# First layer of a four-layer network on one core: key norms applied to the taps' sums, and TensorE's products regrouped by tile shape

## The chip, the cores and the metric

One Trainium2 chip, of which one core is used. The metric is the device time of one execution in microseconds (us). TensorE is called PE in the profile, VectorE DVE, ScalarE ACT, GpSimd POOL, and SyncE, which issues the DMAs, SP.

## The reference

The network has four layers, each `x = x + layer(norm(x))`, on two images of 512 channels and 64 x 64 points, in f32. Only the first layer is touched: local attention over a 3 x 3 window, with 8 heads of 64 channels, joined with attention over 256 pooled tokens.

```
q = x W_q + b_q ;  k, v = split(x W_kv + b_kv)
q_norm   = q / |q|                                  # per head and point
q_scaled = (q_norm + query_embedding) * softplus(temperature)
k_l      = k / |k|                                  # per head and point
attn_local[n, t] = q_scaled[n] . k_l[n + tap t]     # 9 taps, zero outside the image
attn_pool[n, p]  = q_scaled[n] . k_pool[p]          # 256 pooled keys
a = softmax([attn_local, attn_pool])
lt = q_norm . learnable_tokens + bias + a_local
out = sum_t lt[n, t] v[n + tap t] + a_pool v_pool   # then a projection
```

A key's inverse norm is one number per head and point, so `q . (k / |k|)` equals `(q . k) / |k|`: it can multiply the key's 64 channels, or the sum over the channels.

## The kernel before

The class `Local` computes the layer. The image's 512 channels are 4 chunks of 128 (two heads each), and each chunk's 4096 points are 4 units of 1024 points; so there are 16 units (`UT` = 1024 points, two halves of `TB` = 512). `run` works in turns. In turn i it projects keys for unit i+4 and queries for unit i+3 (each two products groups of four 128 x 128 x 512 products, L134), and values for unit i+1. It finds the inverse norms of what the turn before projected (`norms`), multiplies them in (`normed`), forms the tap products and sums of unit i+1 (`tap_products`, `tap_sums`), attends for unit i (`attend`), and weighs the values of unit i-1 (`weigh`, ten steps). Turns 1 to 11 are `steady`. Each of these is a generator, and `in_turn` takes one step of each in the order of the list `stages`. In steady turns TensorE's instructions keep the order in which they are written; the other engines, and TensorE elsewhere, are ordered by a scheduler.

- `norms`: four 128 x 32 products sum the squares per head (L2395), DVE transposes the sums, finds 1/sqrt by three Newton steps, and transposes back into rows of the buffer `sq[1]` (L2410).
- `normed`: a product of 2 rows by 128 columns spreads each row over a head's 64 channels (L2422, one pair for keys, one for queries), and DVE multiplies (L2430). For keys the result goes into `kx`, a frame of 66 x 66 points with a zero border; raw keys lie in `kraw`, queries in `qn`. `learned` (L2445) then multiplies the queries with the learnable tokens.
- `tap_products`: DVE multiplies the queries `qs` with `kx` shifted by the tap, two taps per instruction in steady turns (L2473). `tap_sums`: 128 x 32 products sum over channels into one bank `tap` (L2500), in four strips: two halves of the unit, and even and odd taps. ACT takes the exponential (L2508).
- `attend`: scores against pooled keys (L2525, 64-row products), exponentials (L2529), pooled values (L2535, 64 columns), POOL adds (L2544), sums for the softmax (L2551 and L2554, called P below), their reciprocals on DVE (L2579 to L2587), and the weights' way through a DRAM buffer `rows` (L2592).
- `weigh`: per tap, a fetch spreads the weights over 64 partitions (L2610, two DMAs, three buffers in turn), ACT copies them to a PSUM bank (L2626), DVE multiplies with the values `vx` (L2634), POOL adds (L2639).

All of SP's DMAs stand in one queue. PSUM has 5 banks named `mm` for everything here but the taps' sums and `qs`; a product can only start once its bank's last reader is done.

Of the kernel before, what the change touches and what calls it, by code (L numbers as in the profile page):

```python
# [9 lines left out]
F32 = mybir.dt.float32  # L10
I32 = mybir.dt.int32
AF = mybir.ActivationFunctionType
ALU = mybir.AluOpType
# [1954 lines left out]
class Local:  # L1968
# [9 lines left out]
    def __init__(self, net, X, Y, sp_scale, d, wp, yp, pp, ppt, pps):  # L1978
        self.net, self.nc, self.vec, self.cst = net, net.nc, net.vec, net.cst
        self.X, self.Y, self.sp_scale, self.d = X, Y, sp_scale, d  # L1980
        self.wp, self.pp, self.ppt, self.pps = wp, pp, ppt, pps
        nc, new = self.nc, lambda shape, name: wp.tile(shape, F32, name=name)

        self.yd = yp.tile([P, KC, N], F32, name="yd")
        self.wd = yp.tile([3, P, KC, C], F32, name="wd")
# [37 lines left out]
        self.qb = new([P, KC], "qe_scaled")  # L2023
        self.bias = {i: new([P, KC], "b_" + i) for i in "qkv"}
        self.raw = {"k": self.kraw, "q": self.qn}
# [20 lines left out]
    def run(self):  # L2046
# [8 lines left out]
        for i in "qkv":  # L2055
            self.fetch(i, 0)
        for i in range(-4, units + 1):
            k, q, ahead, u, before = (unit(i + n) for n in (4, 3, 1, 0, -1))
            self.steady = 1 <= i < units - 4
            streams, ended = [], []  # L2060
            stages = [self.norms(streams, ended)]
            if ahead is not None:
                stages.append(self.tap_products(ahead))
            if u is not None:
                stages.append(self.attend(u))
            if i == units:
                stages.append(self.output(KC - 2))
            if before is not None:
                stages.append(self.weigh(before))
            if ahead is not None:  # L2070
                stages.append(self.tap_sums(ahead))
            values = ([ahead] if i > 0 and ahead is not None else
                      {-4: [0], -2: [1]}.get(i, []))
            stages.append(self.projections(k, q, values, streams))
            stages.append(self.normed(ended))
            if i < -2:
                stages.append(islice(heads, 12 if i == -4 else None))
            if i == units - 3:
# [14 lines left out]
    def pooled_tokens(self):  # L2093
# [13 lines left out]
        for blk in range(NB):  # L2107
# [14 lines left out]
            if 1 <= blk <= 3:  # L2122
# [5 lines left out]
                                  self.sq[i], self.vec[:, at:at + KC])  # L2128
                nc.sync.dma_start(self.wd[i], w3)
        self.frame(self.kx)  # L2130
        return xs

    def pooled_heads(self, xs):
# [212 lines left out]
        self.net.project(ps, self.w[which], self.X, blk)  # L2346
        return ps

    def projections(self, uk, uq, uvs, streams):

        nc = self.nc

        def project(u, which, j):
# [20 lines left out]
        for step in range(10):  # L2374
            if step in made:
                i = made.index(step)
                project((uk, uq)[i // 2], "kq"[i // 2], i % 2)
            if step in taken and values:
                u, j = values.pop(0)
                self.value(u, j)  # L2380
                if j and self.last(u):
                    self.fetch("v", u // self.UN + 1)
            yield

    def norms(self, streams, ended):
# [25 lines left out]
        ended += [(s, rows[32 * s:32 * s + 2, :], *a) for s, a in enumerate(before)]  # L2411
        yield

    def normed(self, ended):

        nc = self.nc
        for _ in range(3 if self.steady else 5):
            yield
        for which in "kq":
            mine = [(e, self.bank()) for e in ended if e[2] == which]  # L2420
            for (s, rows, *_), ps in mine:
                nc.tensor.matmul(ps, self.cst[32 * s:32 * s + 2, C_ROW:C_ROW + P], rows, start=True,  # L2422
                                 stop=True)
            for (_, _, _, u, j, part, _), ps in mine:
                out = part
                if which == "k":
                    y = 1 + u % self.UN * self.UY + j * self.UY // 2
                    out = self.kx[:, y:y + self.UY // 2, 1:W + 1]
                    part, ps = (a.rearrange("p (y x) -> p y x", x=W) for a in (part, ps))
                self.multiplied = nc.vector.tensor_tensor(out, part, ps, ALU.mult).ins  # L2430
            yield
        if self.steady:
            yield
        if mine:
            self.learned(mine[-1][0][3])
        yield

    def learned(self, u):

        nc, cc, qn = self.nc, u // self.UN, self.raw["q"]  # L2440
        ps = self.bank()
        for j in range(2):
            for g in range(2):
# [8 lines left out]

    def value(self, u, j):
        ps = self.projected("v", u % self.UN * 2 + j)
        y = 1 + u % self.UN * self.UY + j * self.UY // 2
        self.nc.scalar.activation(self.vx[:, y:y + self.UY // 2, 1:W + 1],
                                  ps.rearrange("p (y x) -> p y x", x=W), AF.Identity,
                                  bias=self.bias["v"][:, u // self.UN:][:, :1])

# [2 lines left out]
    def tap_products(self, u):  # L2462
# [5 lines left out]
        for k in range(0, 9, 2) if self.steady else range(9):  # L2468
# [3 lines left out]
            with held:  # L2472
# [10 lines left out]
    def shifted(self, y, k, n):  # L2483
# [2 lines left out]
        at = lambda k: k // 3 * (W + 2) + k % 3  # L2486
        part, rows, cols = a.ap
        return bass.AP(a.tensor, a.offset + at(k), [part, [at(k + 1) - at(k), n], rows, cols])

    def tap_sums(self, u):  # L2490

# [5 lines left out]
        for k in range(9):  # L2497
            for j in range(2):
# [13 lines left out]
    def attend(self, u):  # L2512
# [58 lines left out]
            halved(1)  # L2571
        yield
        values(1)
        yield
        if not self.steady:
            yield
        psD = sums()

# [7 lines left out]
        nc.vector.tensor_tensor(el, el, self.recip, ALU.mult)  # L2586
        nc.vector.tensor_tensor(el, el, self.lt.pop(u), ALU.add)  # L2587
        if self.steady:
            yield
        self.spread = self.rows()  # L2590
        for j in range(2):
# [244 lines left out]
```

## Time and profile before

| what | value |
|---|---|
| median of 3 runs | 5038.93 us (5038.33 to 5039.80) |
| the profiled execution | 5044.18 us, its span 5042.3 us |
| busy: PE / DVE / ACT / POOL | 4811.1 / 3078.9 / 1814.7 / 1858.9 us |
| first layer's steady turns, first image | about 316 to 785 us of the span |
| period of a steady turn | 42.54 us |
| PE busy, 400 to 600 us | 196.5 of 200 us |

In a timeline a row is a group of like instructions: start, length, engine, source line, operation, tiles, tile shape (rows * columns of the array), moving operand, number of instructions, and in brackets the idle time before it with what ended it. One f32 product is two instructions on PE. A row's length holds a short overlap with its follower, so that lengths from start to start are used for sums.

### The profile page before, as it was taken

The numbers are of one execution on the slowest core, as the hardware profiler recorded it, in microseconds if no ns is written. First come the engines' busy times: TensorE is split into PE (matmuls) and PEld (weight loads), VectorE is DVE, ScalarE is ACT, GpSimd is POOL, SyncE is SP. The second block draws the span as 40 slices with busy tenths as digits, with TensorE's granted clock in tenths as the row PEclk, the third lists the DMA queues.
The fourth block names the chain that finished last, engine by engine and source line by source line (L and its number), as shares of the span: only waits on it lengthen the run. The fifth ranks groups of instructions, "written<-read, shape, count | busy, mean of one in ns | idle before, by whom it ended". The sixth has DMA issues, their size and how long they took to land. (4 is left out here: it accounts for less than half of the span.)

```text
span 5042.3 us, 48033 instructions
## 1 busy us (share of the span) xinstructions
PE 4811.1 (95%) x17027; PEld 1980.8 (39%) x17027; DVE 3078.9 (61%) x4020; ACT 1814.7 (36%) x3477; POOL 1858.9 (37%) x1218
## 2 busy tenths in 40 slices
PE   7999999999999999999999999999999999999998
PEld 3433332555334444433343333335543344444333
DVE  4267777754679633477733677777436795334776
ACT  1245555334323233322112555552443232333221
POOL 0036666501320145454500466664014101554554
PEclk9999999999999999999999999999999999999999
DMA  3035556600000000211120355565000000000111
GB/s 153 0 80 147 148 145 176 168 19 10 1 17 0 2 1 1 69 57 44 57 74 0 101 148 148 145 181 142 19 10 1 17 1 1 1 1 24 40 45 45
DMA packets 124172, 307.72 MB, mean 61 GB/s; under 512 B 20818, under 2 KB 33618, under 8 KB 122388
## 3 DMA queue, kind: packets, MB, share of 16 engines
q1 hardware_dynamic: 123924, 304.58, 20.9%
q8 instruction: 136, 2.23, 0.2%
q14 instruction: 112, 0.92, 0.1%
HBM read 256.01 MB, written 48.50 MB: 60 GB/s over the span
## 5 line engine op out<-in xcount | busy, mean ns | idle before, releaser
L134 PE MATMUL mm<-big,w 128*128 128x512 f32 x2496 | 1175.1, 614 | 30.1 <-DVE big L2430 11.7
L134 PEld LDWEIGHTS mm<-big,w 128*128 128x128 f32 x2496 | 455.3, 192 | 715.7 <-issue 553.0
L2639 POOL TENSOR_TENSOR late<-late,big 128x1024 f32<-128x1024 f32 x194 | 460.2, 2372 | 232.9 <-DVE big L2634 201.5
L2473 DVE TENSOR_TENSOR prods<-qs,big 128x1024 f32<-128x1024 f32 (+1 forms) x200 | 334.1, 1686 | 76.5 <-PE tap L2500 66.3
L1669 POOL TENSOR_TENSOR big<-big 128x512 f32<-128x512 f32 x224 | 278.0, 1273 | 219.0 <-ACT big L1660 219.0
L2634 DVE TENSOR_TENSOR big<-big,mm 128x512 f32<-128x512 f32 x388 | 254.7, 681 | 121.4 <-ACT mm L2626 120.6
L2626 ACT COPY mm<-big 128x512 f32<-128x512 f32 x432 | 248.1, 597 | 107.6 <-DMA big<-rows 59.0
L1660 ACT ACTIVATE big<-mm,ed 128x256 f32<-128x256 f32 x512 | 194.1, 490 | 233.0 <-DVE top L1656 200.3
L2544 POOL TENSOR_TENSOR late<-late 128x512 f32<-128x512 f32 x84 | 105.5, 1277 | 432.2 <-ACT late L2529 410.1
L2639 POOL TENSOR_TENSOR late<-late,tap 128x1024 f32<-128x1024 f32 x94 | 222.3, 2364 | 98.8 <-DVE tap L2634 79.9
L1472 POOL TENSOR_TENSOR wq<-prob 128x512 f32<-128x512 f32 x48 | 71.8, 1518 | 488.1 <-ACT prob L1469 476.7
L1656 DVE TENSOR_REDUCE top<-mm 128x1 f32<-128x512 f32 x256 | 159.0, 683 | 148.1 <-PE mm L1587 148.1
L1924 PE MATMUL mm<-k,w 128*128 128x512 f32 x512 | 236.6, 605 | 12.4 <-DVE k L1917 7.5
L134 PE MATMUL mm<-big,wq 128*128 128x512 f32 x512 | 236.7, 608 | 2.7 <-ACT off_t L1243 2.7
L1382 PE MATMUL acc<-big,diag 128*128 128x512 f32 x512 | 229.0, 605 | 9.8 <-ACT diag L1387 4.6
L1215 PE MATMUL mm<-big,wo 128*128 128x512 f32 x512 | 238.1, 611 | 0.0
L1634 PE MATMUL mm<-w,big 128*128 128x512 f32 x512 | 234.4, 601 | 0.0
L973 POOL TENSOR_TENSOR group_stats<-group_stats,cst 128x1 f32<-128x1 f32 (+1 forms) x20 | 20.2, 1027 | 564.6 <-DVE group_stats L972 508.2
L1914 DVE RECIPROCAL psD<-psD 128x512 f32<-128x512 f32 x64 | 215.1, 3362 | 1.9
L134 PE MATMUL mm<-big,big 128*128 128x512 f32 x464 | 201.7, 594 | 0.5 <-DVE b_sr L1011 0.5
L1469 ACT ACTIVATE prob<-mm 128x512 f32<-128x512 f32 x256 | 133.4, 602 | 171.6 <-PE mm L1466 171.3
L1556 POOL TENSOR_TENSOR sq<-k 128x512 f32<-128x512 f32 x128 | 133.1, 1042 | 155.2 <-ACT k L1554 139.1
(425 smaller groups left out, 8219.2 us busy)
## 6 DMA issues: line engine op xcount, KB each, us to landing
big<-rows SPq DMA_DIRECT2D x432, 256.0 KB, 4.2
tap<-rows SPq DMA_DIRECT2D x208, 256.0 KB, 4.1
yd<-late SPq DMA_DIRECT2D x32, 512.0 KB, 3.1
lost_all<-lost SPq DMA_DIRECT2D x128, 128.0 KB, 3.1
out<-big SPq DMA_DIRECT2D x64, 256.0 KB, 2.0
big<-in_W_kv SPq DMA_DIRECT2D x8, 1024.0 KB, 10.3
rows<-late SPq DMA_DIRECT2D x64, 128.0 KB, 3.6
big<-in_x SPq DMA_DIRECT2D x32, 256.0 KB, 3.6
```

Of the source, the lines that this page charges most:

```text
L134: self.nc.tensor.matmul(ps, w[:, kc, :], X[:, kc, blk * TB:(blk + 1) * TB], start=(kc == 0), stop=(kc == KC - 1))
L1215: nc.tensor.matmul(ps, w[:, kc, oc * P:(oc + 1) * P], att[:, kc, :], start=(kc == 0), stop=(kc == KC - 1))
L1382: nc.tensor.matmul(accs[b], dg, src[:, b * TB:(b + 1) * TB], start=(j == 0), stop=(j == 6))
L1634: nc.tensor.matmul(ps, X[:, kc, lo:lo + P], wv[:, kc, :], start=(kc == 0), stop=(kc == KC - 1))
L1660: nc.scalar.activation(f[:, t, :], pS[h][i][:, t % 2, :], AF.Exp, bias=ed[:, t, 2 * cc + h:2 * cc + h + 1])
L1669: nc.gpsimd.tensor_tensor(a, a, part, ALU.add)
L1914: nc.vector.reciprocal(psD, psD)
L1924: nc.tensor.matmul(ps, self.wo[:, kc, oc * P:(oc + 1) * P], qs[:, kc, :], start=(kc == 0), stop=(kc == KC - 1))
L2473: self.nc.vector.tensor_tensor(self.pair(u, k)[:, :n].rearrange("p k (y x) -> p k y x", x=W), bcast(qs.rearrange("p (y x) -> p y x", x=W), ...
L2626: nc.scalar.copy(ps, part)
L2634: nc.vector.tensor_tensor(part.rearrange("p (y x) -> p y x", x=W), self.vx[:, y:y + self.UY // 2, dx:dx + W], ps.rearrange("p (y x) -> p y ...
L2639: nc.gpsimd.tensor_tensor(out, out, t, ALU.add)
```

## The change

Keys are no longer multiplied by their inverse norms. ACT writes the raw projected keys straight into `kx`. The inverse norms of keys go by DMA into a DRAM buffer `inverse`, per chunk six rows (three copies of two heads), with zeros at both ends. `tap_inverses` reads them back in twelve DMAs of 6 rows x 512, each shifted as its taps are, into a 128 x 512 buffer (the place of `kraw`), and DVE multiplies the taps' sums by it in PSUM before the exponential. Keys are projected one turn later, with the queries of the same unit. In steady turns the stages' order and their steps are moved: `norms` after `attend`, tap sums of taps 4 to 7 in one step next to the learned product, pooled values next to the sums, and the three projections of the last steps behind one another.

```diff
@@ run
-            k, q, ahead, u, before = (unit(i + n) for n in (4, 3, 1, 0, -1))
+            made, ahead, u, before = (unit(i + n) for n in (3, 1, 0, -1))
...
-            stages = [self.norms(streams, ended)]
+            norms = self.norms(streams, ended)
+            stages = [] if self.steady else [norms]
...
                 stages.append(self.attend(u))
+            if self.steady:
+                stages.append(norms)
...
-            stages.append(self.projections(k, q, values, streams))
-            stages.append(self.normed(ended))
+            last = [self.projections(made, values, streams), self.normed(ended)]
+            stages += reversed(last) if self.steady else last
@@ pooled_tokens
+        nc.gpsimd.memset(self.kraw[:, :TB], 0.0)
+        for at in (0, self.edge - 1 + N):
+            nc.sync.dma_start(self.inverse[:, at:at + self.edge + 1],
+                              self.cst[:6 * KC, :self.edge + 1])
@@ projections
-            part = self.raw[which][:, j * TB:(j + 1) * TB]
-            nc.scalar.activation(part, ps, AF.Identity, bias=b)
+            if which == "q":
+                part = self.qn[:, j * TB:(j + 1) * TB]
+                nc.scalar.activation(part, ps, AF.Identity, bias=b)
+            else:
+                part = None
+                nc.scalar.activation(self.rows_of(self.kx, u, j),
+                                     ps.rearrange("p (y x) -> p y x", x=W), AF.Identity, bias=b)
@@ norms
+        for s, (which, u, j, part, _) in enumerate(before):
+            row = rows[32 * s:32 * s + 2, :]
+            if which == "q":
+                ended.append((s, row, u, j, part))
+                continue
+            at = self.edge + 1 + u % self.UN * self.UT + j * TB
+            a = self.inverse[u // self.UN * 6:][:2, at:at + TB]
+            heads, cols = a.ap
+            nc.sync.dma_start(bass.AP(a.tensor, a.offset, [heads, [2 * heads[0] - 1, 3], cols]),
+                              bcast(row, 1, 3))
@@ normed
-        for which in "kq":
-            mine = [(e, self.bank()) for e in ended if e[2] == which]
...
+        mine = [(e, self.bank()) for e in ended]
...
+        for (*_, part), ps in mine:
+            self.multiplied = nc.vector.tensor_tensor(part, part, ps, ALU.mult).ins
+        for _ in range(2):
             yield
@@ tap_products
-            for _ in range(n):
+            for _ in range(1 if self.steady and k > 2 else n):
                 yield
@@ tap_inverses (new)
+        inverse = (self.kraw[:, :TB] if u < KC * self.UN - 1
+                   else self.w3[:, 2].rearrange("p k o -> p (k o)"))
+        for q in range(4):
+            for dy in range(3):
+                at = u % self.UN * self.UT + q // 2 * TB + dy * W + 1
+                self.nc.sync.dma_start(inverse[32 * q + 6 * dy:][:6, :],
+                                       self.inverse[u // self.UN * 6:][:6, at:at + TB])
+        return inverse
@@ tap_sums
+            if k == 3:
+                inverse = self.tap_inverses(u)
             if k % 2:
-                for _ in range(((2, 2, 3, 1) if self.steady else (2, 2, 2, 1))[k // 2]):
+                for _ in range(((2, 2, 0, 1) if self.steady else (2, 2, 2, 1))[k // 2]):
                     yield
+        nc.vector.tensor_tensor(ps, ps, inverse, ALU.mult)
         el = self.els()
         nc.scalar.activation(el, ps, AF.Exp)
@@ attend, after values(1)
-        yield
         if not self.steady:
             yield
+            yield
         psD = sums()
...
         if self.steady:
+            yield
             yield
         self.spread = self.rows()
```

In the changed kernel these lines have other numbers: L2395 becomes L2413, L2422 L2448, L2430 L2451, L2473 L2492, L2500 L2530, L2525 L2558, L2535 L2568, L2551 and L2554 L2584 and L2587, L2634 L2668; new are L2437 (write of inverse norms), L2516 (read) and L2539 (the multiply of the sums).

More of the change, by code (lines that the diff above doesn't have):

```diff
@@ L1984, in __init__ @@
         self.yd = yp.tile([P, KC, N], F32, name="yd")
+        self.edge = W + 1
+        self.inverse = yp.tile([6 * KC, N + 2 * self.edge], F32, name="inverse")
         self.wd = yp.tile([3, P, KC, C], F32, name="wd")
@@ L2024, in __init__ @@
         self.bias = {i: new([P, KC], "b_" + i) for i in "qkv"}
-        self.raw = {"k": self.kraw, "q": self.qn}
         self.w, self.lt, self.el, self.out = {}, {}, {}, {}
@@ L2347, in projected, with rows_of, projections, project @@
         return ps
-    def projections(self, uk, uq, uvs, streams):
+    def rows_of(self, a, u, j):
+        y = 1 + u % self.UN * self.UY + j * self.UY // 2
+        return a[:, y:y + self.UY // 2, 1:W + 1]
+    def projections(self, u, uvs, streams):
         nc = self.nc
-        def project(u, which, j):
+        def project(which, j):
             if u is None:
@@ L2376, in projections @@
                 i = made.index(step)
-                project((uk, uq)[i // 2], "kq"[i // 2], i % 2)
+                project("kq"[i // 2], i % 2)
             if step in taken and values:
[L2379 to L2382, printed above, removed]
+                v, j = values.pop(0)
+                self.value(v, j)
+                if j and self.last(v):
+                    self.fetch("v", v // self.UN + 1)
             yield
@@ L2410, in norms @@
         nc.vector.transpose(rows, ps)
-        ended += [(s, rows[32 * s:32 * s + 2, :], *a) for s, a in enumerate(before)]
+        for s, (which, u, j, part, _) in enumerate(before):
[8 more added lines that the diff above has]
+                              bcast(row, 1, 3))
         yield
@@ L2418, in normed @@
             yield
-        for which in "kq":
-            mine = [(e, self.bank()) for e in ended if e[2] == which]
[L2421 to L2430, printed above, removed]
-            yield
-        if self.steady:
+        mine = [(e, self.bank()) for e in ended]
+        for (s, rows, *_), ps in mine:
+            nc.tensor.matmul(ps, self.cst[32 * s:32 * s + 2, C_ROW:C_ROW + P], rows, start=True,
+                             stop=True)
+        for (*_, part), ps in mine:
+            self.multiplied = nc.vector.tensor_tensor(part, part, ps, ALU.mult).ins
+        for _ in range(2):
             yield
         if mine:
-            self.learned(mine[-1][0][3])
+            self.learned(mine[-1][0][2])
         yield
     def learned(self, u):
-        nc, cc, qn = self.nc, u // self.UN, self.raw["q"]
+        nc, cc, qn = self.nc, u // self.UN, self.qn
         ps = self.bank()
@@ L2454, in value @@
         ps = self.projected("v", u % self.UN * 2 + j)
-        y = 1 + u % self.UN * self.UY + j * self.UY // 2
-        self.nc.scalar.activation(self.vx[:, y:y + self.UY // 2, 1:W + 1],
+        self.nc.scalar.activation(self.rows_of(self.vx, u, j),
                                   ps.rearrange("p (y x) -> p y x", x=W), AF.Identity,
@@ L2488, in shifted, with tap_inverses @@
         return bass.AP(a.tensor, a.offset + at(k), [part, [at(k + 1) - at(k), n], rows, cols])
+    def tap_inverses(self, u):
+        inverse = (self.kraw[:, :TB] if u < KC * self.UN - 1
[6 more added lines that the diff above has]
+        return inverse
     def tap_sums(self, u):
@@ L2573, in attend @@
         values(1)
-        yield
         if not self.steady:
+            yield
             yield
```

## The prediction

> **What bounds the kernel now.** I read the page's 40 slices first, then the busy time by stretch, then TensorE's own timeline.
>
> ```profile
> PE   7999999999999999999999999999999999999998
> L134 PE MATMUL mm<-big,w 128*128 128x512 f32 x2496 | 1175.1, 614 | 30.1 <-DVE big L2430 11.7
> ```
>
> ```profile
> 400.00:600.00 200.00, 196.51 (x719) 61.21 (x718) 151.03 (x235) 119.15 (x212) 122.90 (x63) 1.00 0.55 149
> ```
>
> TensorE (PE) is busy in every slice, and in the first layer's middle for 196.5 of 200 us, against 151.0 for VectorE (DVE), 119.2 for ScalarE (ACT) and 122.9 for GpSimd (POOL). So TensorE's work and its switches are what counts there, but DVE at 76% can become the next bound. One turn of the steady stage, in TensorE's timeline (start, length, group; two instructions make one f32 product):
>
> ```profile
> 544.36 1.06 PE L2500 MATMUL tap<-prods,cst 128*32 128x512 f32 x8
> 545.35 1.13 PE L2422 MATMUL mm<-sq,cst 2*128 2x512 f32 x4
> 546.41 1.13 PE L2525 MATMUL mm<-big,kp 64*128 64x512 f32 x4
> 548.06 3.70 PE L134 MATMUL mm<-big,w 128*128 128x512 f32 x8 [0.53 <-DVE big L2430]
> 551.70 1.13 PE L2422 MATMUL mm<-sq,cst 2*128 2x512 f32 x4
> 552.75 1.94 PE L2535 MATMUL mm<-late,vp 128*64 128x512 f32 x8
> ...
> 558.49 3.70 PE L134 MATMUL mm<-big,w 128*128 128x512 f32 x8
> 562.12 1.06 PE L2445 MATMUL mm<-big 128*32 128x512 f32 x8
> 563.12 3.70 PE L134 MATMUL mm<-big,w 128*128 128x512 f32 x8
> 566.75 1.07 PE L2500 MATMUL tap<-prods,cst 128*32 128x512 f32 x8
> ```
>
> The same groups return every 42.54 us (548.06, then 590.61). Almost all follow without a gap; a turn's gaps are 0.53 us (on DVE) and 0.17 us (on ACT), so 41.84 us of a turn is TensorE's own. There are 23 groups of differing tile shape in a turn.
>
> [...] two neighbouring groups of one shape are shorter than two apart.
>
> ```profile
> 274.85 7.13 PE L134 MATMUL mm<-big,w 128*128 128x512 f32 x16
> 826.98 1.92 PE L2500 MATMUL tap<-prods,cst 128*32 128x512 f32 x16
> ```
>
> Two projections apart take 2 x 3.63 us from start to start, side by side 7.06 (274.85 to 281.91): 0.20 us less. Two tap groups apart take 2 x 1.00, side by side about 1.86 (1.92 less the overlap of 0.07 at its end): 0.14 less. [...] ACT's copies of taps stand behind activations that wait for PE (DVE L2634 waits up to 2.4 us for them). [...] the 16 KB write `lost<-half` lands after 1.9 us.
>
> **The change, part by part.** I took the order of instructions and each wait's producer from the changed program as built, and all durations from the profile of before.
>
> *Keys' scaling.* 64 of the 128 L2422 products go: 32 pairs of 1.06 us, 11 in each image's steady turns and 5 outside. 64 DVE multiplies of 0.68 us go and 32 come (L2539, tap sums times inverse norms, 0.7 us by the like L2634): DVE gains 0.7 us a turn. New on SP's queue: in each turn 2 writes of inverse norms and 12 reads of 12 KB. A tap fetch takes 0.55 us to issue[...].
>
> *Side by side.* In a steady turn the projections stand in 4 groups, not 6 (2 x 0.20); the 32-column products in 3, not 7 (4 x 0.14); the last values join the sums (0.16). That is 1.12 us; with the keys' pair 2.18. TensorE's own turn becomes 41.84 - 2.18 = 39.66 us.
>
> *New waits.* The turn's end is now: sums (P), tap products 4 to 7 with the learned product, tap 8, three projections (k1, q0, q1). q1 needs the PSUM bank of weighing step 7, so DVE's multiply of that step. DVE's list after P, with lengths from this view:
>
> ```profile
> 558.61 0.73 DVE L2579 STREAM_TRANSPOSE mm<-mm 128x512 f32<-128x512 f32 x1 [0.20 <-PE mm L2554]
> 559.37 0.37 DVE L2581 RECIPROCAL mm<-mm 128x32 f32<-128x32 f32 x1
> 559.77 0.72 DVE L2582 STREAM_TRANSPOSE late<-mm 128x512 f32<-128x512 f32 x1
> 560.53 0.95 DVE L2586 TENSOR_TENSOR late<-late 128x512 f32<-128x512 f32 x1
> 561.51 0.69 DVE L2587 TENSOR_TENSOR late<-late 128x512 f32<-128x512 f32 x1
> ...
> 567.88 2.29 DVE L2473 TENSOR_TENSOR prods<-qs,big 128x2048 f32<-128x2048 f32 x1 [1.40 <-PE tap L2500]
> ```
>
> From P's end: transpose and reciprocal 1.2; tap product 8 (1.2, it waits for the products of 4 and 5) 2.4; transpose 3.1; weighing step 6 and the two small ops 5.9; the next unit's first pair (2.2) 8.1; L2539 8.8; second pair 11.0; only then step 7, done at 11.7. In before, step 7 came ahead of these pairs. TensorE would start q1 at 3.6 + 3.6 + 3.4 = 10.6: **1.1 us of wait**. ACT feels it too: its exponential of the taps waits for L2539 at 8.8, with steps 7 to 9 and the activations of q0 and q1 behind it. q1's activations end at 16.4 and the next projection, which takes q1's bank, could start at 16.2: 0.25 us. Step 7's late multiply makes its POOL add end at 14.7; then the next unit's first tap is fetched (0.55 issue, 4.2 to land, page part 6), copied and multiplied at 21.4; the norms' product, which takes that bank, could start at 21.1: 0.35 us. The 0.53 us at L2430 stays (same groups around it), the 0.17 goes: its bank now belongs to another step, free in time. Turn: 42.54 - 2.18 - 0.17 + 1.1 + 0.25 + 0.35 = 41.9; following one whole turn with these rows gives 41.8. I take **41.8, 0.74 less; 22 turns: 16 us less**.
>
> *SP's queue.* The reads stand behind the fetch of tap 6 and ahead of taps 7 to 9; they wait until the second write has landed (1.9). They start some 4.6 us before P and, at 0.55 us each, end 2 us after it; the fetch of tap 7, due at POOL's add 4 (about P), may slip 2 us and land at 7.5, used at 9.5. So I cost the 14 transfers at nothing; the cover is the waits of weighing for POOL, and without it each us goes onto the turn. The queries' next weights, fetched once q1 has ended, stand ahead of the first tap's fetch in 2 turns of an image: +1 us each, 4 us.
>
> *Outside the steady turns.* 10 pairs of 1.06 (10.6); one norms group less per image (2.0); before the first query the wait of 2.45 us at 204.86 for keys' norms goes (4.9), since no norms are due there; the pooled heads lose a projection that covered DVE's 2.8 us at 167.5, some 1.5 us per image (3.0). Net 14.5 less; between nothing and 20, as the fill and drain turns also have waits of 1 to 4 us whose place may move. Two memsets and four writes of zeros once per image lie beside the first projections: nothing.
>
> **Sum.** -16 + 4 - 14.5 = -26.5. The profiled execution took 5044.18 us (span 5042.3), so 5017.7 on its own scale; it stands 5.25 above the median 5038.93, and on the median's scale this is **5012**.
>
> **Rivals.** (A) as above, 5012, own range 4995 to 5028: 52%. (B) The new waits don't arise, because taps land early and DVE runs ahead: turn 40.2, 51 less, with 14.5 outside: 4973. For it: DVE idles some 10 us in a turn now. Against it: DVE's order is fixed and its idle time is elsewhere. 18%. (C) Slower: L2539 holds DVE. [...] ACT's exponential waits for it. It decides when the 12 reads land later than 8.1 us after P; by my upper price (0.55 each) they land near 6.2, 1.9 us of slack. From there on each us is a us per turn. Break-even is a turn of 43.0 (0.48 x 22 + 4 - 14.5 = 0), so reads landing 1.2 us beyond the point; 2 us beyond gives 43.8, 28 - 10.5 = 17 more: 5056. For it: a fetch's first tap already takes 4.2 us to land and weighing fills the whole turn. Against: the reads are small. 22%. (D) waits give back just what switches save outside my places: within 10 us of before. 8%. That the change doesn't regroup TensorE is excluded by the built order, which shows 15 groups in a steady turn.
>
> **Numbers.** What a measurement of this kernel can tell from no change is about 0.2%, 10 us. Faster by more: most of A, all of B: 0.65; within: 0.13; slower: 0.22. Range 4972 to 5056: from B's value, to C's.
>
> **What would show it.** A turn's period near 41.8 in the timeline; an idle of about 1 us before the third projection of the row put down to DVE big; some 0.3 us before the norms' product; L2539 without a wait for DMA. Wrong: a turn over 42.5, or DVE waiting at L2539 for the reads, or ACT waiting long at the exponential of the taps; or a turn near 40, where the wait at q1 is not there.

## The result, and the profile after

The changed kernel took **5024.89 us** (median of 8 runs, 5015.68 to 5028.05), the kernel before 5039.89 beside it: 0.9966 of it, 95% interval 0.9957 to 0.9976. It is 15 us faster. A repeat (e1 below) gave 0.9963 (0.9952 to 0.9974), 19 us. Forecast were 5012 and a range from 4972 to 5056.

The page of the changed kernel, with TensorE's slices and its costliest group (busy, mean ns, idle before, releaser); then the busy times of the same 200 us (PE, PEld, DVE, ACT, POOL, granted clock, DMA share, GB/s):

```profile
PE   7999998999999999999999999989999999999998
L134 PE MATMUL mm<-big,w 128*128 128x512 f32 x2496 | 1160.8, 610 | 30.7 <-DVE big L2451 10.3
```

```profile
400.00:600.00 200.00, 192.70 (x706) 65.44 (x707) 147.21 (x221) 123.72 (x217) 127.07 (x63) 0.99 0.58 153
```

TensorE is still what bounds the first layer, with 192.7 of 200 us in place of 196.5: it has less work, but it waits more. Its clock column reads 0.99, where it read 1.00. One turn in TensorE's timeline shows where both are:

```profile
491.44 1.07 PE L2587 MATMUL mm<-late,cst 64*64 64x512 f32 x4
492.45 1.92 PE L2530 MATMUL tap<-prods,cst 128*32 128x512 f32 x16
494.19 1.04 PE L2465 MATMUL mm<-big 128*32 128x512 f32 x8
495.05 1.03 PE L2530 MATMUL tap<-prods,cst 128*32 128x512 f32 x4
496.01 7.13 PE L134 MATMUL mm<-big,w 128*128 128x512 f32 x16
503.54 3.67 PE L134 MATMUL mm<-big,w 128*128 128x512 f32 x8 [0.40 <-DVE tap L2668]
...
508.57 3.70 PE L134 MATMUL mm<-big,w 128*128 128x512 f32 x8 [0.30 <-ACT sq L2379]
...
523.25 1.13 PE L2448 MATMUL mm<-sq,cst 2*128 2x512 f32 x4 [0.32 <-ACT late L2562]
524.31 1.13 PE L2558 MATMUL mm<-big,kp 64*128 64x512 f32 x4
525.72 5.40 PE L134 MATMUL mm<-big,w 128*128 128x512 f32 x8 [0.28 <-DVE big L2451]
```

The groups of one shape stand side by side (492.45, 496.01), one pair of 2-row products is left (523.25), and the third projection waits 0.40 us for VectorE, not the 1.1 forecast. The last projection took 5.40 us in place of 3.70, though its eight instructions follow one another: here TensorE's granted clock was 0.5 for 3.41 us (from 526.14). The turns are no longer alike. In the first image they took 42.54 us each before (the first one 42.77); now they take 40.35 to 43.23, 41.55 in the mean.

Where the time went is read from marks in the timelines: the products P that end a turn's sums (L2554 before, L2587 after) and the second layer's first product. "Start" is the time to an image's first P, "end" the time from the twelfth P to the second layer. In us, from one profiled execution of each kernel:

| kernel | start 1 | 11 turns | end 1 | layers 2 to 4, start 2 | 11 turns | end 2 | rest | span |
|---|---|---|---|---|---|---|---|---|
| before | 302.0 | 468.2 | 271.5 | 1762.6 | 468.5 | 274.0 | 1495.6 | 5042.3 |
| after | 285.2 | 457.1 | 284.3 | 1751.6 | 457.5 | 285.8 | 1492.5 | 5013.9 |
| e3 regrouping alone | 300.0 | 469.9 | 278.1 | 1763.7 | 469.5 | 277.2 | 1494.5 | 5052.8 |
| e6 the same, 32 rows | 301.7 | 460.7 | 278.0 | 1760.3 | 460.5 | 276.0 | 1494.1 | 5031.2 |
| e9 keys alone, mended | 286.7 | 456.5 | 285.1 | 1751.3 | 456.6 | 284.0 | 1498.6 | 5018.7 |
| e12 after, no reads | 285.1 | 448.8 | 276.0 | 1746.4 | 448.4 | 276.0 | 1495.3 | 4975.9 |

In the changed kernel two key projections (2 x 3.63 = 7.3 us) have moved from each image's start to its end, since keys are projected a turn later. Taking that out, the two starts won 9.5 and 3.7 us, the 22 turns 22.1, and the two ends lost 5.5 and 4.5. This is bookkeeping and not yet a cause: e4 below puts these projections back, and the ends don't get shorter.

The profile shows 28 us of gain, the medians 15 to 19. The execution profiled before is slower than the median of its kernel, the one after is the fastest of its eight. Mean granted clock was 0.984 in the one of before (31 stretches at half clock) and 0.986 in the one of after (26). In the kernel before, time and clock go together from one execution to the next: of the 21 runs of before beside e1, those at 0.986 and 0.987 took 5035.1 to 5036.1 us, with one of 5039.2, those at 0.984 took 5040.5 to 5045.4. In the changed kernel they do so only in part: its eight runs at 0.984, here and in e1, took 5015.0 to 5028.1 us.

### The profile page after: what moved, and what is told of

The parts are those of the page before. It is cut to its first block, busy times and chain, and to the rows that moved or that the text cites. A ratio compares the mean times of both kernels' runs of the same rounds, so it can differ in the third digit from the quotient of the medians.

```text
span 5013.9 us, 48352 instructions
## 1 busy us (share of the span) xinstructions
PE 4752.0 (95%) x16883; PEld 1985.0 (40%) x16883; DVE 3035.2 (61%) x3958; ACT 1818.7 (36%) x3477; POOL 1866.6 (37%) x1220
## 5 line engine op out<-in xcount | busy, mean ns | idle before, releaser
L134 PE MATMUL mm<-big,w 128*128 128x512 f32 x2496 | 1160.8, 610 | 30.7 <-DVE big L2451 10.3
L2492 DVE TENSOR_TENSOR prods<-qs,big 128x1024 f32<-128x1024 f32 (+1 forms) x200 | 331.5, 1684 | 49.8 <-PE tap L2530 29.2
L2668 DVE TENSOR_TENSOR big<-big,mm 128x512 f32<-128x512 f32 x388 | 254.9, 679 | 113.2 <-ACT mm L2660 97.7
L2530 PE MATMUL tap<-prods,cst 128*32 128x512 f32 x1152 | 185.0, 613 | 24.5 <-ACT late L2541 20.7
```

What stands on the lines that cost most here:

```text
L134: self.nc.tensor.matmul(ps, w[:, kc, :], X[:, kc, blk * TB:(blk + 1) * TB], start=(kc == 0), stop=(kc == KC - 1))
L2492: self.nc.vector.tensor_tensor(self.pair(u, k)[:, :n].rearrange("p k (y x) -> p k y x", x=W), bcast(qs.rearrange("p (y x) -> p y x", x=W), ...
L2668: nc.vector.tensor_tensor(part.rearrange("p (y x) -> p y x", x=W), self.vx[:, y:y + self.UY // 2, dx:dx + W], ps.rearrange("p (y x) -> p y ...
```

## The experiments

Two theories stood at the outset. Mine: the keys' pair and the regrouping each save what was counted, less some waits. The rival: the gain is one of them alone, or the new transfers eat part of it.

### e1: the changed kernel again

> The changed kernel unaltered, for a second profile and for the spread of its runs. The first profiled execution took 5015.7 us, ten less than the median of 5024.9, and had two stretches of about 3.4 us at half clock in the steady turns (one an image). Theory 1 (each execution catches a different number of such stretches, and each costs 1.7 us): median 5022 to 5027, the profile's steady turns as before (41.4 to 41.7 us each), but with more half-clock stretches, about 4 to 8 more for 10 us. Rival (the times differ through DMA landings or engine waits): the same number of stretches and longer waits, above all of the products that wait for VectorE.

Measured: 5020.44 us (7 runs, 5014.99 to 5031.8). The profiled run took 5016.5 us and had 26 half-clock stretches, as many as the first, so it caught none of the long executions, and counting in the profile decides nothing. Over the runs the clock speaks for theory 1 at the edges (0.986 at 5016.5 us, 0.982 at 5031.8), but not in between (four runs at 0.984 took 5015.0 to 5022.3). What spreads the runs stays open.

### e2, e5 and e9: the keys' part alone

> The keys' part alone: the inverse norms multiply the taps' sums, but the stages of turns 1 to 11 stand in the order and steps of the kernel before, so that products of different tile shapes stay mixed. Theory (the prediction's sum): 32 products with their change of tile shape go, 1.06 us a pair, 22 pairs in the steady turns and the rest in the ramp, less the multiplication of the sums as a new link: 12 to 20 us below before, 5020 to 5028, steady turns 41.5 to 42.0. Rival 1 (the pair's time is only filled by waits, since VectorE is as loaded as it was): 5035 to 5042. Rival 2 (the transfers of the inverse norms get in the way, and the regrouping alone brings the gain): slower than before, 5045 or more.

```diff
-            stages = [] if self.steady else [norms]
+            stages = [norms]
...
-            for _ in range(1 if self.steady and k > 2 else n):
+            for _ in range(n):
...
-        for _ in range(3 if self.steady else 5):
+        for _ in range(4 if self.steady else 5):
             yield
         mine = [(e, self.bank()) for e in ended]
```

(and so on for every step that the change moves). Measured: 5092.15 us, 1.0101 (1.0084 to 1.0118) of before. No expectation held: the time is what rival 2 gave, but it is not the transfers that TensorE waits for. TensorE's timeline of e2:

```profile
455.30 1.13 PE L2556 MATMUL mm<-big,kp 64*128 64x512 f32 x4
459.44 5.37 PE L134 MATMUL mm<-big,w 128*128 128x512 f32 x8 [3.02 <-ACT late L2560]
```

The last projection of a turn waits for an exponential. Such waits come to 35.7 us in 11 turns, of which 1.9 stand at another projection that has them before, too. Some of the gaps are followed by half clock (5.37 us for 3.70). The five `mm` banks would explain it. Before, two key norm products lay between the last pairs of scores (L2525), and the projection took the bank of one of them, which VectorE cleared after 0.53 us. Without them it would take a bank whose exponential ScalarE has only just been given. The trace names no banks, so this is tested by edits.

> The keys' part alone as in e2, with two PSUM banks of the ring of five skipped in each of turns 1 to 11, where the keys' two norm products took them before. Theory (e2 is slow because without those two banks the values' second projection gets the bank of exponentials that ScalarE has only just been given, 35.7 us of TensorE's idle time in 11 turns, and the half-clock stretches follow from these gaps): that wait goes, the turns fall from 45.9 to 41.5 to 42 us, the time to 5015 to 5035. Rival (the wait has another cause, such as ScalarE running late through the multiplication of the taps' sums): 5070 or more.

```diff
+        for _ in ended if self.steady else ():
+            self.bank()
         mine = [(e, self.bank()) for e in ended]
```

Measured: 5096.50 us, the wait unchanged at 35.6 us. Most likely the edit did not do what it was meant to: a bank that nothing writes was not passed over, and the banks stayed as in e2. By itself it tells nothing of the cause; the next edit reaches the same end by order.

> The keys' part alone as in e2, with the queries' pair of norm products a step earlier in turns 1 to 11, where the keys' pair stood, so that it comes between the two last pairs of the values' exponentials and the last projection again. Theory (the five PSUM banks: in e2 and e5 the last projection gets the bank of an exponential issued just ahead of it and waits 3.0 us for ScalarE; before, and with this edit, it gets the bank of a norm product, which VectorE clears after about 0.5 us): the wait of 1.6 us a turn and the half-clock stretches behind it go, the turns fall from 45.6 to about 41.5 (42.54 less one pair of 1.06), and with the ramp's 15 us an image won and 12 lost at its end the time is 5008 to 5025. Rival (TensorE waits for ScalarE because ScalarE itself is late, through the multiplication of the taps' sums ahead of its exponential): turns of 44 us or more, 5070 or more.

```diff
-        for _ in range(4 if self.steady else 5):
+        for _ in range(3 if self.steady else 5):
             yield
         mine = [(e, self.bank()) for e in ended]
...
-        for _ in range(2):
+        for _ in range(3 if self.steady else 2):
             yield
```

Measured: 5023.08 us, 0.9967 (0.9954 to 0.9980). TensorE's timeline of e9:

```profile
524.73 1.13 PE L2446 MATMUL mm<-sq,cst 2*128 2x512 f32 x4
525.79 1.13 PE L2556 MATMUL mm<-big,kp 64*128 64x512 f32 x4
527.44 3.70 PE L134 MATMUL mm<-big,w 128*128 128x512 f32 x8 [0.52 <-DVE big L2449]
```

The queries' pair now stands where the keys' stood, the wait is 0.52 us and again VectorE's, and the turns take 41.48 us (the first 41.7): 42.54 less exactly one pair of 1.06. So the 69 us between e2 and e9 were the price of one place in the order of banks, with the half-clock stretches behind its gaps (14 in e2's 22 turns, none in e9's). **The keys' part alone gives what the whole change gives** (0.9967, against 0.9966 and 0.9963).

### e3, e6 and e7: the regrouping, and the clock

> The regrouping alone: the keys are normalised by the products and multiplications of before, but the stages of turns 1 to 11 stand as in the changed kernel (taps' sums first, norms behind them, both pairs of norm products side by side, three projections in a row). Theory (the prediction's sum): 1.12 us of changes of tile shape less a turn, 22 turns, 25 us, less new waits at the third projection and at the norms of 0.6 to 1.6 us a turn: 5015 to 5042. Rival 1 (regrouping brings nothing, or its waits eat it, and the keys' pair is all of the gain): 5040 to 5060, steady turns 42.5 or more. The two parts add up to the whole if the gains of this and of the keys' part alone come to 15 us.

The edit is the change's own reordering of stages and steps applied to the kernel before, with both norm pairs side by side:

```diff
                 self.multiplied = nc.vector.tensor_tensor(out, part, ps, ALU.mult).ins
-            yield
-        if self.steady:
-            yield
+            if not self.steady:
+                yield
+        if self.steady:
+            yield
+            yield
```

Measured: 5051.50 us, 1.0024 (1.0015 to 1.0033): slower than before. Half of the 22 turns take 41.87 us, 0.67 less than before, but about every second one takes 43.5. Two neighbouring turns of e3:

```profile
543.47 1.06 PE L2505 MATMUL tap<-prods,cst 128*32 128x512 f32 x8
544.47 1.42 PE L2425 MATMUL mm<-sq,cst 2*128 2x512 f32 x8
545.98 1.72 PE L2530 MATMUL mm<-big,kp 64*128 64x512 f32 x4
548.38 5.36 PE L134 MATMUL mm<-big,w 128*128 128x512 f32 x8 [0.67 <-DVE big L2433]
...
588.00 1.42 PE L2425 MATMUL mm<-sq,cst 2*128 2x512 f32 x8
589.51 1.72 PE L2530 MATMUL mm<-big,kp 64*128 64x512 f32 x4
591.90 3.70 PE L134 MATMUL mm<-big,w 128*128 128x512 f32 x8 [0.67 <-DVE big L2433]
```

The groups and the wait are the same; only the projection differs, 5.36 and 3.70. The busy times of the two stretches around 548 us (granted clock is the third number from the end):

```profile
543.47:548.38 4.91, 4.15 (x23) 1.35 (x21) 3.83 (x7) 1.76 (x5) 2.32 (x1) 1.00 0.71 179
548.38:553.66 5.28, 5.28 (x8) 2.08 (x8) 5.28 (x4) 3.19 (x5) 2.54 (x3) 0.68 0.35 99
```

All recorded stretches of half clock last 3.41 us or a multiple, except the last of each profile, which its end cuts short; the granted clock in them is 0.5. In the profiles of before and after, all of their starts (31 and 26) lie whole multiples of 3.4133 us apart, to within 0.001 us (from 165.511 to 5039.744 in before: 1428 times). So the traces were cut into intervals of that length. In e3's turns TensorE had products under way for 0.62 to 0.84 of the interval before a halved stretch, so these intervals were far from idle. Shares of the array in use were therefore estimated from the traces. An instruction of 512 columns counts for 0.43 us, which is the time from one start to the next in a row of projections. It is weighted by the part of the array that it uses. In all 14 profiles, from 300 us on, 393 intervals at full clock were followed by a halved one and 18,392 by another at full clock. With rows times columns over 128 x 128 as the weight, 375 of the 393 had a share under 0.36, but so had 93 of the others. With the rows alone (of 128, and products that run at the same time counted together up to 128), 369 of the 393 were under 0.36 and only one of the others. So of these two shares the rows in use tell the intervals ahead of a halved one apart better (misplaced are 24 and 1, against 18 and 93); that columns count is not shown. In the first layer's turns the two shares hardly differ. In e3's turns the share ahead of a halved stretch is 0.26 to 0.29 (once 0.36 to 0.37): the stretch from 544.5 to 548.4 us, with two pairs of products that use 2 of 128 rows and a wait of 0.67, falls into one interval in every second turn.

> The regrouping alone as in e3, but each product that spreads the inverse norms contracts over 32 rows, 30 of them times zero, in place of 2. It takes as long and gives the same sums, but uses sixteen times as much of TensorE's array. Theory (a stretch of 3.41 us in which less than about 0.36 of the array is used is followed by one at half clock; in e3 two pairs of such thin products side by side and a wait behind them fill a stretch in every second turn, 11 stretches in the steady turns at 1.7 us each): these stretches go, turns of 41.9 throughout, 15 to 19 us less than e3, 5032 to 5037. Rival (it is idle time that lowers the clock, or a busy share of any kind): the stretches stay, 5048 to 5056.

```diff
-                nc.tensor.matmul(ps, self.cst[32 * s:32 * s + 2, C_ROW:C_ROW + P], rows, start=True,
+                nc.tensor.matmul(ps, self.cst[32 * s:32 * s + 32, C_ROW:C_ROW + P], rows, start=True,
```

Measured: 5027.26 us, 0.9975 (0.9966 to 0.9983): 24 us less than e3, more than the 15 to 19 expected. The same place in e6:

```profile
541.93 1.42 PE L2425 MATMUL mm<-sq,cst 32*128 32x512 f32 x8
543.44 1.72 PE L2530 MATMUL mm<-big,kp 64*128 64x512 f32 x4
545.84 3.70 PE L134 MATMUL mm<-big,w 128*128 128x512 f32 x8 [0.67 <-DVE big L2433]
```

Same length of the products, same wait, more rows, and no half-clock stretch in any of the 22 turns, where e3 had ten; the lowest share is 0.41. Since the waits are the same (0.67 us), idle time alone is excluded as the cause of these ten, and the number of rows in use (2 or 32) is shown to matter here. And the regrouping's own worth is seen: 41.87 for 42.54.

> The changed kernel with the queries' products over 32 rows in place of 2, as in e6. Theory (share of the array used): at most the one or two half-clock stretches of the steady turns go, 1.7 us each: 5015 to 5024, 0 to 5 us below the changed kernel. Rival (idle time decides): no difference, steady turns with one or two half-clock stretches an image.

The edit is the same line in the changed kernel. Measured: 5016.82 us, 0.9954 (0.9940 to 0.9967), no half-clock stretch in the 22 turns. Its interval overlaps those of the changed kernel, so a gain of 4 to 8 us is possible but not shown.

### e4, e8, e10 and e12: what the ends lose

> The changed kernel with the keys projected a turn earlier, as before the change (four units ahead, not three). Theory (the image's last turns lose 6 us because with one unit's keys more in turn 12 the multiplication of the taps' sums comes late to ScalarE's exponential, whose one bank the next sums wait for): the 7.3 us of the two projections move back ahead of turn 1, and the last turns get shorter by 7.3 plus up to 6 us an image: 5013 to 5025. Rival (the loss at the end belongs to the multiplication and the reads themselves, wherever the keys are made): same as the changed kernel within 3 us, the last turns shorter by 7.3 us only, the turns ahead of 1 longer by as much.

```diff
-            made, ahead, u, before = (unit(i + n) for n in (3, 1, 0, -1))
+            uk, made, ahead, u, before = (unit(i + n) for n in (4, 3, 1, 0, -1))
...
-                project("kq"[i // 2], i % 2)
+                project((uk, uq)[i // 2], "kq"[i // 2], i % 2)
```

Measured: 5024.82 us. The first start became 7.2 us longer, the second did not (1750.6 us), and the ends stayed at 285.0 and 284.3 us. The theory fell: the moved projections are not what lengthens the ends.

> The keys four units ahead as in e4, and in the turns outside 1 to 11 the twelve reads of the inverse norms issued at the head of the turn, not behind the fourth product of the taps' sums (the inverse norms that they take were written a turn earlier, since the keys are). Theory (the planner places the multiplication late on VectorE since its reads come late; the single bank of the taps' sums is then held and TensorE idles 12.7 us in two places of an image's last turns): the multiplication moves some 12 instructions forward on VectorE in these turns, the idle time in front of the taps' sums goes, 10 to 13 us an image: 5000 to 5010. Rival (the reads' place doesn't matter, VectorE is late with everything in these turns): 5020 to 5028.

```diff
         ps = self.ppt.tile([P, TB], F32, name="tap")
+        if not self.steady:
+            inverse = self.tap_inverses(u)
         yield
...
-            if k == 3:
+            if k == 3 and self.steady:
                 inverse = self.tap_inverses(u)
```

Measured: 5031.40 us. The multiplication came earlier, and TensorE's waits for the exponential at the taps' sums (13.1 us in the first image's end in e4) went, yet the ends stayed at 284.4 and 284.5 us: ScalarE's copies now waited longer for the spread weights, 46.1 us in the first end, against 30.7 in e4 and 17.8 in the changed kernel.

> The changed kernel without the multiplication of the taps' sums by the inverse norms; the twelve reads are still made. The sums stay unscaled: this part of the computation is left out. Theory (the new link between the taps' sums and their exponential costs the last turns of an image 5 us beyond the moved projections, since VectorE comes to it late while the single bank is held; in turns 1 to 11 it is one of VectorE's 0.7 us in front of the third projection's wait): the last turns and the output's first part fall from 285 to 275 to 280 us an image, turns 1 to 11 by 0 to 0.3 us each: 5003 to 5017. Rival (the end of the image is late for its order of instructions, not for this link): 5018 to 5026.

```diff
-        nc.vector.tensor_tensor(ps, ps, inverse, ALU.mult)
```

Measured: 5015.34 us, 0.9950 (0.9935 to 0.9965); the ends at 287.6 and 287.7 us. So leaving the multiplication out wins nothing in the ends. The turns took 450.7 us in the first image, 6.4 less than in the changed kernel, but 457.0 in the second, where three half-clock stretches fell into them. Over the runs the gain is not clear of noise: the interval overlaps those of the changed kernel.

> The changed kernel without the twelve reads a unit that spread the inverse norms; the multiplication is still made, by a tile that holds zeros, so this part of the computation is left out. An image's last turns and the first part of the output took 284 to 288 us in every kernel with the keys' part (also with the keys ahead as before, with early reads, and without the multiplication), 271 to 278 us without it. Theory (SyncE's queue: twelve issues of 0.45 us stand in front of the spread weights' reads, for which ScalarE's copies and then VectorE and GpSimd wait): this stretch falls to 276 to 281 us an image, the time to 5003 to 5014. Rival (the order of the last turns, with one unit's keys more in them, sets it, whatever the transfers): the stretch stays at 284 to 288 us, 5014 to 5022.

```diff
-                self.nc.sync.dma_start(inverse[32 * q + 6 * dy:][:6, :],
-                                       self.inverse[u // self.UN * 6:][:6, at:at + TB])
+                pass
```

Measured: **4981.65 us**, 0.9886 (0.9869 to 0.9902): 39 to 43 us below the changed kernel. Both ends fall to 276.0, the second start becomes 5.2 us shorter, and most turns fall to 40.67, which was not expected at all. SyncE's queue in the changed kernel, in a steady turn and near an image's end (start, length):

```profile
489.02 4.14 SPq L2516 DMA_DIRECT2D big<-inverse  x12
...
829.92 6.38 SPq L2644 DMA_DIRECT2D big<-rows  x4
836.35 5.37 SPq L2516 DMA_DIRECT2D big<-inverse  x12
841.82 1.09 SPq L2644 DMA_DIRECT2D tap<-rows  x2
```

Twelve reads take the queue 4.14 us in the turn and 5.37 near the end, and the next fetch of spread weights (L2644) goes out right behind them. In the turns part of the effect reaches TensorE at the third projection, whose bank a late step of the weighing holds. The three projections in e12, to be held against those at 496.01 and 503.54 above, and then those in e10:

```profile
493.04 10.57 PE L134 MATMUL mm<-big,w 128*128 128x512 f32 x24
...
493.37 10.61 PE L134 MATMUL mm<-big,w 128*128 128x512 f32 x24
```

Both are one row of 24 without a gap. In e10 all twelve reads are still issued, so this wait, 2.8 us in an image's turns, is not the queue's. It is VectorE's order: in the seven turns of the changed kernel that wait, the multiplication (0.7 us) and two pairs of tap products stand ahead of weighing step 7. Without the multiplication step 7 comes 0.6 us earlier (e10, fourth turn). In e12 the multiplication is still there, but from the second turn on the scheduler puts step 7 ahead of both pairs, as it does in the changed kernel in three of the four turns without the wait.

The wait at the norms' products (L2413) is another matter. It comes in two turns of an image, those in which the next weights are fetched, and is 2.7 and 3.1 us in the two images of the changed kernel. It is still 2.4 and 2.6 us in e10 and is gone in e12. In the changed kernel the first tap's multiplication (L2665) is late there because its weights are, so the reads' place in the queue is the likelier cause. The rest of e12's gain in the turns is a half-clock stretch an image (1.7 us) and smaller waits at L2448.

In the ends the changed kernel's largest wait of TensorE, 9.7 and 11.0 us at the taps' sums for the exponential behind the multiplication, is gone in e12. It was gone in e8 and e10, too, and there other waits took its place. So only taking the reads away helps, and the queue is the likelier path; but this is argued, not shown. The theory's own sign is missing in the ends: ScalarE's copies wait there longer for spread weights in e12 than in the changed kernel (31.0 us for 17.8 in the first end). In the first image's turns they wait less, 31.6 us for 43.9.

### e11: the third projection's wait by order

> The changed kernel with the queries' products over 32 rows as in e7, and in turns 3 to 11 the first pair of tap products of the next unit held on VectorE behind the multiplication of weighing step 7, so that the third projection's bank comes free earlier. Theory (the third projection waits 0.2 to 1.1 us in two turns of three because VectorE takes a pair of tap products of 2.3 us ahead of that multiplication): the wait goes, 0 to 7 us below e7: 5008 to 5018. Rival (the tap products, started later, make the taps' sums at the head of the next turn late): the turns grow by up to 1 us, 5018 to 5038.

```diff
+                    else self.net.tc.issue_after(self.seventh) if self.steady and k == 0 and u > 2
```

Measured: 5047.28 us, 1.0013 (1.0006 to 1.0020). It is slower than either expectation. TensorE's timeline:

```profile
413.29 10.57 PE L134 MATMUL mm<-big,w 128*128 128x512 f32 x24
423.79 1.13 PE L2559 MATMUL mm<-big,kp 64*128 64x512 f32 x4
427.00 5.40 PE L134 MATMUL mm<-big,w 128*128 128x512 f32 x8 [2.08 <-DVE tap L2669]
```

The wait at the third projection went, as the theory had it: the three projections are one row of 24. But a wait of 2.08 us came at the projection after them, where the changed kernel waits 0.30 for ScalarE, in seven turns of the first image. In five of these a half-clock stretch followed, and they took 44.15 us. VectorE's list shows why: with the first pair of tap products held behind step 7, the second pair (2.29 us, from 423.47) now stands ahead of a later multiplication of the weighing (from 425.67), for which this projection waits. VectorE's delay was moved to the next bank, not removed. The rival's place, the taps' sums, shows no wait.

## Why the prediction was right, and where it was not

Direction and range were right, and 5012 was 13 us too low (8 by the repeat). Against the two profiled executions, 28 us apart, the forecast sum of 26.5 even fits, but that is luck: two large errors of opposite sign lie inside. The turns won 22 us where 12 had been counted, and everything outside them 3 where 14.5 had been.

- **The keys' pair**, 1.06 us: exact (e9, 41.48 for 42.54).
- **The regrouping**, 1.12 us: right. It was reckoned from the lengths of neighbouring groups in the trace of before (0.20 and 0.14 us less side by side); why they take less is not shown. TensorE's own time in a turn, the period less all its idle time, was 41.84 before and 40.72 in e6 (41.87 less 1.15, of which 0.18 are gaps too short for the timeline to print). For both parts together it is 39.76 in most turns of e12, where 39.66 had been forecast.
- **The new waits**: the one at the next projection was 0.30 a turn (0.25 forecast). The third projection's was mis-sized: 0.40 us in seven of the 11 turns of each image and nothing in the other four, 0.26 in the mean, not 1.1. In a turn that waits step 7 was done 10.9 us after P's end, where 11.7 had been counted, and in three turns it came ahead of the tap products. The 0.35 a turn at the norms' product came in another form: L2413 waited only in the two turns with the weights' fetch, 1.07 and 1.62 us in the first image and 2.05 and 1.03 in the second, which is rather the weights' term (1 us each). The L2448 products add some 0.1 a turn. The turn came to 41.55, not 41.8.
- **SP's queue at nothing**: this step failed. In the steady turn shown the reads take even less time in the queue than was counted (4.14 us for 6.6) and end 1.7 us after P, where 2 had been counted (489.02 to 493.16, P at 491.44). But the cover that was named, the waits of weighing for GpSimd, was not enough. Without the reads the kernel is 39 to 43 us faster, 8 to 9 us of it in each image's turns, and 8 to 10 in each end. Not all of this is the queue: 2.8 us of each image's turns come from VectorE's order (e10). The queue had been followed through one steady turn only, and the turns with the weights' fetch and the ends are where it tells.
- **Outside the steady turns**, 14.5 less: 13.2 us came at the starts, but the ends gave 10 back, net 3.2. The ends were counted by what is removed, not by what the twelve reads delay.
- **Rival C** had the right suspects, the reads and L2539 ahead of the weighing, but the wrong way: a multiplication that waits for its data. L2539 left VectorE no gap put down to a DMA; what cost time was its place and length on VectorE (0.69 us at 499.92 in the turn shown, ahead of step 7 at 502.72), and what stands behind the reads.
- **Not thought of**: the clock. With the keys' pair kept, the regrouping loses more by half clock than it wins (e3: 5051.50 us with ten such stretches in the 22 turns, e6 5027.26 with none, before 5039.3 beside both). In the changed kernel one such stretch an image is left in the turns.

Keys alone and the whole change measure the same, so the regrouping brings nothing on top of the keys' part as it stands: 457 us for 11 turns in both. What it saves (40.67 for 41.48 in the best turns) is spent on waits that the fixed 42.54 us of before did not have.

## What to carry to other kernels

Cost a small DMA by its time in the queue, by what stands behind it there and by where it makes the scheduler put the instruction that uses it, in every stage, not by its bytes: twelve reads of 12 KB took 4 to 5.4 us of the queue a unit, and the kernel without them is some 40 us faster. Where one engine's order sets a wait, look for the next bank that waits for the same engine: holding one instruction back moved the wait and made it longer (e11). Before a product is removed or moved, ask whose PSUM bank the next one will then get: here one pair's place was worth 69 us. When thin products are put side by side, look at the granted clock as well as at the groups' lengths; here using more rows of the array, with zeros, cost no time (1.42 us in both) and left no half-clock stretch in 22 turns, where there had been ten (e6, e3).

## What the hardware showed that was not expected

Half clock (0.5) came within busy stretches too (5.28 us of work in the 5.28 us at 548.38 in e3), in whole intervals of 3.41 us. In the 14 profiles it went with the estimated share of the array's rows in use in the interval before (below about 0.36 in 369 of 393 cases, and in one of 18,392 others); e3's ten were not a matter of idle time alone, since e6 has the same wait of 0.67 us and none. Contracting over 32 rows in place of 2 left the products' length at 1.42 us and took all ten such stretches out of the 22 turns. Two parts of a change, as first taken apart, were each slower alone than the kernel before (1.0101 and 1.0024) and faster together (0.9966); what ties them is the order of banks (e9) and the clock (e6).
